# Block 3's keys and values from the context ahead of time, and four heads in a lone pass

## The chip, the cores and the metric

The kernel runs on one core of one Trainium2 chip. A core has five engines that run side by side: TensorE (PE, matrix products), VectorE (DVE), ScalarE (ACT), GpSimd (POOL) and SyncE (SP, which only issues transfers). [...] Products land in PSUM, everything else is in SBUF or in DRAM. The metric is the device time of one launch, in microseconds (us).

## The reference, cut to what matters

A batch of 8 sequences of 512 tokens, 256 features, goes through two layers, each an attention-like block and a feed-forward block, all gated by a tanh:

```python
x = x + tanh(g_xattn[0]) * mlstm(layernorm(x), ctx, ctx, ...)         # block 1: 8 heads of 32, decay matrix
x = x + tanh(g_ffn[0])   * attn_experts(layernorm(x), ...)            # block 2: self-attention, 32 heads of 8, then experts
x = x + tanh(g_xattn[1]) * cross(ctx, ctx, layernorm(x), mask, ...)   # block 3: 16 heads of 16
x = x + tanh(g_ffn[1])   * product_keys(layernorm(x), ...)            # block 4: top-8 of 4096 experts

def cross(k, v, q, mask, Wq, bq, Wk, bk, Wv, bv, Wo, bo):             # k = v = ctx
    qh = split_heads(q @ Wq + bq) / sqrt(16)
    kh, vh = split_heads(k @ Wk + bk), split_heads(v @ Wv + bv)
    scores = where(mask, einsum('bhqd,bhkd->bhqk', qh, kh), -inf)
    return einsum('bhqk,bhkd->bqhd', softmax(scores), vh).reshape(...) @ Wo + bo
```

The keys and values of block 3 depend on the context alone, not on `x`.

## The kernel before, in words

Everything is float32. The kernel has two stages: the attention stage (blocks 1 to 3, and the first products of block 4), which ends about 3078 us into the span, and the retrieval stage (the rest of block 4).

In the attention stage the sequences are taken in the order 0, 4, 1, 5, 2, 6, 3, 7 and are called m = 0 to 7. The two softmax attentions are cut into 24 *jobs*: ("A", m, f), f = 0 or 1, is half of block 2's heads of sequence m, ("C", m, 0) is block 3 of it. A job has 16 steps n = (g, c): group g of four heads, 128 rows c. Each job is passed twice. In the first pass (`maxima`) PE makes scores with queries on the partitions and DVE reduces them to row maxima (`nm`, L435). In the second pass (`exponentials`) PE makes the scores the other way round, with the maximum folded in as a further row of the operand, ACT takes the exponential from PSUM (`pr`, L463), and `values` multiplies with the values (`av`, L478). A head has at most 32 rows of operand, so four heads fit on PE's four groups of 32 rows and run side by side.

A hand-written planner interleaves the jobs. One round of its loop takes one step of the first pass of one job and one step of the second pass of the job before it, each in two half rounds. In a half round the first pass takes heads 2*half and 2*half + 1, the second the other two, so a full round always has four heads on PE. Each of the two passes takes one of the two score buffers in PSUM (`ps_sc`, two of 128 x 2 x 512) in a half round. Where one pass has no partner (the first job's maxima, the last job's exponentials, or a job that isn't ready), a half round has two heads alone. Between the score groups the planner hands PE time (`CREDIT`, in its own units) to *lanes*: generators that make the other blocks and say after each piece how much PE time it took or for how long they want to be left alone. The order of the lanes is their priority:

- `between` spreads a job's queries and keys from DRAM into the sets of operands `qa`, `ka` (`spread`);
- `after` closes block 3 (`leave`), and ends with `norm`;
- `before` makes block 1 (`cell`) and block 2's queries, keys and values (`queries`), in one lane for m = 0, 1, 3 to 7, and in a second lane, with borrowed tiles (`Lent`), for m = 2;
- `behind` makes the experts of block 2 (`experts`), then block 3's operands: `operands` projects keys from the context and queries from the stream, writes both to DRAM and spreads them; `values1` projects block 3's values straight into `v1`, after the block 3 before it has finished with `v1`;
- `fill` makes products of block 4 (`inner`, line L131) and has the lowest priority.

`weights2` fetches the projection weights of `behind` one ahead. `load_context` loads a transposed context into a tile "cT" (one buffer) on POOL's queue. The store tiles `pk`/`vk` share two buffers. PE's order is exactly the order of emission (`manual_schedule`); the order on the other engines is made by the framework's scheduler from the dependences.

Of the kernel before, what the change touches and what calls it, by code (L numbers as in the profile page):

```python
# [21 lines left out]
P = 128  # L22
# [14 lines left out]
def kernel(  # L37
# [142 lines left out]
    def attention_phase(ctx: ExitStack):  # L180
# [6 lines left out]
        wsp = ctx.enter_context(tc.tile_pool(name="wsp", bufs=2))  # L187
# [51 lines left out]
        class Weights:  # L239
# [20 lines left out]
        operand = [(w0, 3), (w3, 1), (w3, 0)]  # L260
        weights2 = Weights(
            "ws2", (M - 2) * (operand + [(w3, 2)]) + 2 * operand + 2 * [(w3, 2)], wsp
        )
# [56 lines left out]
        m_f = trp.tile([B * NC, P], F32, name="m_f", tag="pk", bufs=2)  # L320
        nc.vector.tensor_copy(m_f, m_u8)
# [3 lines left out]
        def constants():  # L325
# [8 lines left out]
            nc.vector.tensor_scalar(tbo, tbo, tg[:, 2:3], None, ALU.mult)  # L334
            mp = ps_m.tile([P, S], F32, name="mp", tag="m")
# [69 lines left out]
        class Attention:  # L405
            def __init__(self, m, qa, ka, va, first, hd):
                self.m, self.qa, self.ka, self.va = m, qa, ka, va
                self.first, self.hd = first, hd
                self.o = None

# [44 lines left out]
            def exponentials(self, n, half):  # L455
                g, c, jj = n // NC, n % NC, 1 - half
                if half == 0:
                    self.pr = [None, None]
                sc, product = self.pair(self.ka, self.qa, g, c, jj)

                def then():
                    self.pr[jj] = prb.tile([P, 2, S], F32, name="pr", tag="pr")
                    nc.scalar.activation(self.pr[jj], sc, AF.Exp)  # L463
                    if half == 1:
                        self.ready = (n, self.pr)

                return product, then

            def values(self):


                n, pr = self.ready
# [43 lines left out]
        xbs, cTs, lnx, qks, vds, xds, weights = {}, {}, {}, {}, {}, {}, {}  # L516
# [30 lines left out]
        class Tiles:  # L547
            user = ""

# [6 lines left out]
            def begin(self, m):  # L556
# [5 lines left out]
                nc.gpsimd.dma_start(qn, x[b].rearrange("(c p) d -> p c d", p=P))  # L562
                cT, ce = self.context(m)
                load_keys(nc.gpsimd, ce, b)
# [17 lines left out]
        class Lent(Tiles):  # L582
            user = "2"

# [13 lines left out]
            def context(self, m):  # L598
                return load_context(m, "cT"), self.cte
# [97 lines left out]
        def cell(m, own):  # L697
            b = order[m]
            qn, cT, ce = own.begin(m)
# [83 lines left out]
            if m == 0:  # L783
                all_pairs(qT, cT, ce, nM_d, aT, close)
            for pair in range(4) if m else ():
# [164 lines left out]
        def experts(m):  # L950
            Xb = xbs[m][:, :, :D]
            cTs[m] = load_context(m, "cTc" if m == M - 1 else "cT")
# [12 lines left out]
            w = weights2.get()  # L965
            for c in range(NC):
                ps = project(w, oT, c)
# [54 lines left out]

        def operands(m):
            Xb, cT = xbs[m][:, :, :D], cTs[m]
            b = order[m]
            xn = trp.tile([P, NC, D], F32, name="xn3", tag="t2")
# [4 lines left out]
            place, free = cross_set(m)  # L1031
            q1, k1 = sets[place]
            for i, srcT, dst in ((1, cT, k1), (0, nT, q1)):
                pd = drm.tile([D, S], F32, name="qk_d3")
                w = weights2.get()
                for n in range(NK):

                    def store(ps):
                        pk = trp.tile([P, S], F32, name="pk", tag="pk", bufs=2)
                        nc.vector.tensor_scalar(  # L1040
                            pk, ps, bqkv_sb[:, 2 * i + n : 2 * i + n + 1],
                            0.25 if i == 0 else 1.0, ALU.add, ALU.mult,
                        )
                        nc.sync.dma_start(pd[n * P : (n + 1) * P], pk)

                    yield from project_T(w, srcT, n, store)
                if i == 1:
                    yield ("rest", free)
                    mrow = m_dram[NC * b : NC * (b + 1)].rearrange("(o c) p -> o (c p)", o=1)
                    for j in range(4):  # L1050
                        for g in range(4):
                            nc.sync.dma_start(k1[32 * j + 16 : 32 * j + 17, g, :], mrow)
                    blank(q1)
                spread(dst, pd, 0, 16)

        def values1(m):
            b = order[m]
            vv = v1[:, :, : 16 * 17].rearrange("p c (h e) -> p c h e", e=17)
            w = weights2.get()
            for c in range(NC):  # L1060
                mk = m_key[:, NC * b + c : NC * b + c + 1]
                ps = project(w, cTs[m], c)
                nc.vector.tensor_scalar(
                    vv[:, c, :, 0:16], ps.rearrange("p (h e) -> p h e", e=16), mk, None, ALU.mult
                )
                nc.gpsimd.tensor_scalar(vv[:, c, :, 16], ones[:, :16], mk, None, ALU.mult)
                yield 1.0
# [132 lines left out]
        def before(sequences, tiles):  # L1200
            if tiles is Lent:
                yield ("rest", ("begun", 0))
            own = tiles()
            for m in sequences:
                Xa = yield from cell(m, own)
# [10 lines left out]
        def behind():  # L1216
            yield ("rest", ("lent", 0))
            for m in range(M):
# [10 lines left out]
                for n in (m,) if m < M - 2 else (m - 1, m) if m == M - 1 else ():  # L1229
# [627 lines left out]
```

## Time and profile before

| | |
|---|---|
| median of 3 runs | 3934.26 us (3929.36 to 3937.77) |
| the profiled execution's own time | 3939.58 us |
| its span | 3937.6 us |
| mean granted PE clock | 0.956 |
| attention stage | 0 to 3078 us |
| first job's maxima, alone | 114 to 255 us |
| last job's exponentials, alone | from 2921 us |
| PE busy | 3599.6 us |
| DVE busy | 2244.4 us |
| ACT busy | 1760.8 us |

The profile's page gives the busy time of each engine over the whole span; since the stages have different limits, the stretches between the planner's jobs are to be looked at one by one. The granted clock is the share of PE's full clock that it was given[...]. A busy PE includes matmuls that use only a part of its array.

### The profile page before, as it was taken

How to read it: one execution, taken by the hardware profiler on the slowest of the kernel's cores; microseconds unless marked ns; L12 is line 12 of the kernel's file. 1: busy time of each engine (PE TensorE's matmuls, PEld its weight loads, DVE VectorE, ACT ScalarE, POOL GpSimd, SP SyncE). 2: the span in 40 equal slices, each digit the busy share in tenths (PEclk: the TensorE clock that was granted, in tenths of full speed). 3: DMA queues.
4: the chain of work that ended last, by engine and by line, in shares of the span. 5: the costliest groups of instructions: out<-in, count | busy, mean ns of one | idle time of the engine just before them, and what ended most of it. 6: DMA issues, size and time to landing. Idle time of an engine off the chain costs nothing.

```text
span 3937.6 us, 76092 instructions
## 1 busy us (share of the span) xinstructions
PE 3599.6 (91%) x31049; PEld 1853.6 (47%) x31049; DVE 2244.4 (57%) x5483; ACT 1760.8 (45%) x2304; POOL 608.9 (15%) x645
## 2 busy tenths in 40 slices
PE   4898899898999999889999989988899999999998
PEld 1333344343343444334444434424344677777776
DVE  4546655655555554555444453455321589999993
ACT  2223544444444454444444443444244355555652
POOL 4003112111101110101100100010000133333331
PEclk7658999999999999999999999999899999999999
DMA  3203122131322332222332323220433443333331
GB/s 102 80 28 103 55 69 85 39 93 46 96 82 77 89 94 90 76 87 76 89 107 86 98 67 99 75 55 25 129 110 119 116 121 104 105 104 116 114 103 37
DMA packets 226249, 339.04 MB, mean 86 GB/s; under 512 B 30110, under 2 KB 175550, under 8 KB 217598
## 3 DMA queue, kind: packets, MB, share of 16 engines
q1 hardware_dynamic: 208476, 274.35, 23.5%
q0 software_dynamic: 16288, 59.25, 5.1%
q8 instruction: 244, 4.00, 0.4%
q14 instruction: 105, 0.86, 0.1%
q10 hardware_dynamic: 1136, 0.58, 0.1%
HBM read 236.66 MB, written 96.63 MB: 85 GB/s over the span
## 4 chain that ended last, share of the span: by engine, by line
PE 78%; DVE 11%; issue 3%; ACT 3%; DMA 2%; POOL 1%; SPq 0%; DVEq 0%; POOLq 0%; ACTq 0%
PE sc L417 22%; PE acc L1699 12%; PE ps_hd L131 10%; DVE nm L435 7%; PE av L478 7%; PE cf L1679 4%; PE ps_y L1003 3%; PE ps_sim L1431 3%; PE ps_p L366 3%; PE ps_q L377 3%; PE ps_h L984 3%; PE csc L826 2%; PE cav L811 1%; PE ps_hl L131 1%; PE ps_t L347 1%
## 5 line engine op out<-in xcount | busy, mean ns | idle before, releaser
L435 DVE TENSOR_REDUCE nm<-sc 128x2 f32<-128x1024 f32 x768 | 940.8, 1225 | 1046.5 <-PE sc L417 1045.8
L463 ACT ACTIVATE pr<-sc 128x1024 f32<-128x1024 f32 x768 | 786.1, 1024 | 999.0 <-PE sc L417 998.5
L417 PE MATMUL sc<-ka,qa 32*128 32x512 f32 x3072 | 974.1, 672 | 138.6 <-DVE nm L435 119.8
L417 PE MATMUL sc<-qa,ka 32*128 32x512 f32 x3072 | 899.8, 657 | 24.8 <-ACT pr L463 24.0
L417 PEld LDWEIGHTS sc<-ka,qa 32*128 32x128 f32 x3072 | 266.4, 191 | 527.5 <-DVE nm L435 310.7
L1699 PE MATMUL acc<-up_sb,gs 64*128 64x256 f32 x4096 | 468.4, 382 | 1.3 <-DVE gs L1688 1.3
L131 PE MATMUL ps_hd<-xT,dw 128*64 128x256 f32 x3584 | 430.5, 386 | 10.2 <-DVE pd L831 5.8
L478 PE MATMUL av<-pr,v 128*32 128x512 f32 x3072 | 424.4, 625 | 1.1 <-ACT pr L463 1.1
L1699 PEld LDWEIGHTS acc<-up_sb,gs 64*128 64x128 f32 x4096 | 390.0, 187 | 52.4 <-issue 4.7
L131 PEld LDWEIGHTS ps_hd<-xT,dw 128*64 128x64 f32 x3584 | 242.2, 137 | 233.1 <-issue 98.9
L1669 POOL TENSOR_TENSOR m<-o,cwT 128x1024 f32<-128x1024 bf16 x128 | 243.6, 1903 | 562.4 <-DVE o L1667 241.3
L417 PEld LDWEIGHTS sc<-qa,ka 32*128 32x128 f32 x3072 | 243.9, 187 | 80.2 <-ACT pr L463 54.2
L1163 ACT COPY hb<-ps_hd 128x512 f32<-128x512 f32 x224 | 131.3, 586 | 306.8 <-PE ps_hd L131 283.1
L478 PEld LDWEIGHTS av<-pr,v 128*32 128x32 f32 x3072 | 61.3, 109 | 305.1 <-issue 291.0
L804 ACT ACTIVATE pd<-mb,aT 128x256 f32<-128x256 f32 (+2 forms) x224 | 113.1, 553 | 184.8 <-PE cav L811 100.6
L1688 DVE TENSOR_TENSOR gs<-cf,gs 128x1024 f32<-128x1024 f32 x128 | 155.8, 1219 | 42.4 <-PE cf L1679 27.3
L1679 PE MATMUL cf<-m,m 64*64 64x64 f32 x8192 | 152.4, 222 | 0.8 <-DVE gs L1688 0.7
L1679 PEld LDWEIGHTS cf<-m,m 64*64 64x64 f32 x8192 | 134.8, 135 | 38.7 <-issue 38.3
L1665 ACT CAST m<-o 128x1024 f32<-128x1024 bf16 x128 | 133.7, 1045 | 39.3 <-DVE o L1663 35.5
L826 PE MATMUL csc<-qT,cT 32*128 32x512 f32 (+1 forms) x448 | 136.2, 537 | 12.3 <-DVE o L506 5.0
L984 PE MATMUL ps_h<-fT,w1e 128*128 128x256 f32 x512 | 133.7, 397 | 5.4 <-DVE o L506 4.8
L796 POOL TENSOR_SCALAR_AFFINE_SELECT mb<-mb 128x256 f32<-128x256 f32 x112 | 45.7, 408 | 581.7 <-ACT pd L804 347.1
(260 smaller groups left out, 4064.7 us busy)
## 6 DMA issues: line engine op xcount, KB each, us to landing
h_d<-hb SPq DMA_DIRECT2D x224, 256.0 KB
gs<-h_d SPq DMA_DIRECT2D x56, 1024.0 KB
dw<-in_down SPq DMA_DIRECT2D x112, 256.0 KB
qk_d<-pk SPq DMA_DIRECT2D x64, 256.0 KB
w1e<-in_w POOLq DMA_DIRECT2D x16, 1024.0 KB, 5.8
w2e<-in_w POOLq DMA_DIRECT2D x16, 1024.0 KB, 6.5
ws<-in_w SPq DMA_DIRECT2D x56, 256.0 KB
mb<-nM_d SPq DMA_DIRECT2D x28, 512.0 KB
```

The costliest lines, as they stand in the source:

```text
L131: nc.tensor.matmul(ps[64 * q : 64 * q + 64, :], dw[:, k, :], runs[:, :, q, :], start=(k == 0), stop=(k == NK - 1),)
L417: nc.tensor.matmul(sc[:, i, :], lhs[r : r + 32, g, c * P : (c + 1) * P], rhs[r : r + 32, g, :], start=True, stop=True,)
L435: newest = nc.vector.tensor_reduce(self.nm[:, c, 2 * half : 2 * half + 2, g], sc, AX.X, ALU.max, negate=True)
L463: nc.scalar.activation(self.pr[jj], sc, AF.Exp)
L478: nc.tensor.matmul(self.av[32 * j : 32 * j + 32, :], self.va[:, c, h * (self.hd + 1) : h * (self.hd + 1) + 32], pr[j // 2][:, j % 2, :], s ...
L826: nc.tensor.matmul(sc[i][:, s0:], cT[r : r + 32, g, s0 : s0 + P], qT[r : r + 32, g, s0:], start=True, stop=True,)
L984: nc.tensor.matmul(ps[:, :D], w1e[:, k, f * P : (f + 1) * P], fT[:, k, i * D : (i + 1) * D], start=(k == 0), stop=(k == NK - 1),)
L1665: nc.scalar.copy(m1, o1)
L1669: nc.gpsimd.tensor_tensor(m2, o2, tokens(cw), ALU.mult)
L1679: nc.tensor.matmul(cf[64 * q : 64 * q + 64, h, s, :], m2[rows, 4 * q + s // 2, :, s % 2], m1[rows, 4 * q + s // 2, :, s % 2], start=True, ...
L1688: nc.vector.tensor_tensor(gv, cf.rearrange("p h s i -> p i h s"), gv, ALU.mult)
L1699: nc.tensor.matmul(accs[n][q], gs[n % 2][rows, i, :], up_sb[rows, i, :], start=(i == 0), stop=(i == 63),)
```

## The change

Three things are changed together.

1. Block 3's keys and values of all sequences are projected in a lane of their own, `contexts`, above `fill` in priority: the keys of m = 0 to 3, then their values, and, after ("A", 1, 0), the keys and values of m = 4 to 7. They are kept in DRAM (`k_d3`, `v_d3`). `operands` now projects only the queries, then spreads both; `values1` becomes a lane that loads `v1` from DRAM. The weights `wo2` and `wq3` are kept in SBUF for the whole stage instead of being fetched for each use. The context is reloaded for each projection.
2. In a round with one pass alone (`alone`) both half rounds are issued as one, with four heads and both score buffers; the credit of both half rounds is given at once.
3. The second cell (m = 1) is made by the `Lent` lane, and m = 2 by the other. Its loads are issued at once, on SP's queue, and it goes on as soon as the first cell's products (`all_pairs`) are issued, not when the first maxima begin; once the first maxima have begun it stands ahead of the other lanes of `before` and `behind`. The cast of the mask is moved from the head of the stage into `constants`.

```diff
-        wsp = ctx.enter_context(tc.tile_pool(name="wsp", bufs=2))
+        wsp = ctx.enter_context(tc.tile_pool(name="wsp", bufs=1))
...
-        operand = [(w0, 3), (w3, 1), (w3, 0)]
-        weights2 = Weights(
-            "ws2", (M - 2) * (operand + [(w3, 2)]) + 2 * operand + 2 * [(w3, 2)], wsp
-        )
+        wo2, wq3 = (wsp.tile([P, NK, D], F32, name=name) for name in ("wo2", "wq3"))
+        for w, src in ((wo2, w0[3]), (wq3, w3[0])):
+            nc.sync.dma_start(w, src.rearrange("(k p) n -> p k n", p=P))
...
         nc.sync.dma_start(m_u8, mask)
-        m_f = trp.tile([B * NC, P], F32, name="m_f", tag="pk", bufs=2)
-        nc.vector.tensor_copy(m_f, m_u8)
...
             nc.vector.tensor_scalar(tbo, tbo, tg[:, 2:3], None, ALU.mult)
+            m_f = trp.tile([B * NC, P], F32, name="m_f", tag="pk", bufs=2)
+            nc.vector.tensor_copy(m_f, m_u8)
...
         class Lent(Tiles):
             user = "2"
+            loader = nc.sync
...
             def context(self, m):
-                return load_context(m, "cT"), self.cte
+                cT = exp.tile([P, NK, S], F32, name="cT2", tag="xT5", bufs=1)
+                self.loader.dma_start(cT, cxT[order[m]].rearrange("(k p) s -> p k s", p=P))
+                return cT, self.cte
...
                 all_pairs(qT, cT, ce, nM_d, aT, close)
+                rested.add(("pairs", 0))
...
+        def contexts():
+            for half in (range(M // 2), range(M // 2, M)):
+                for i in (1, 2):
+                    if i == 1 and half[0]:
+                        yield ("rest", ("A", 1, 0))
+                    w = wsp.tile([P, NK, D], F32, name="wkv", tag="wkv")
+                    nc.sync.dma_start(w, w3[i].rearrange("(k p) n -> p k n", p=P))
+                    for m in half:
+                        cT = load_context(m, "cT")
+                        yield ("wait", 5 if m or i > 1 else 25)
+                        for cost in (keys3, values3)[i - 1](m, w, cT):
+                            yield cost
+                            yield ("wait", 2)
+        def store3(pd, ps, n, i, scale):
+            pk = trp.tile([P, S], F32, name="pk", tag="pk", bufs=2)
+            nc.vector.tensor_scalar(
+                pk, ps, bqkv_sb[:, 2 * i + n : 2 * i + n + 1], scale, ALU.add, ALU.mult
+            )
+            nc.sync.dma_start(pd[n * P : (n + 1) * P], pk)
+        def keys3(m, w, cT):
+            pd = kds[m] = drm.tile([D, S], F32, name="k_d3", bufs=M)
+            for n in range(NK):
+                yield from project_T(w, cT, n, lambda ps: store3(pd, ps, n, 1, 1.0))
+            rested.add(("k_d", m))
+        def values3(m, w, cT):
+            pd = vcs[m] = drm.tile([P, NC, 16 * 17], F32, name="v_d3", bufs=M)
+            for c in range(NC):
+                mk = m_key[:, NC * order[m] + c : NC * order[m] + c + 1]
+                ps = project(w, cT, c)
+                pk = trp.tile([P, S], F32, name="vk", tag="pk", bufs=2)[:, : 16 * 17]
+                heads = pk.rearrange("p (h e) -> p h e", e=17)
+                nc.vector.tensor_scalar(
+                    heads[:, :, 0:16], ps.rearrange("p (h e) -> p h e", e=16), mk, None, ALU.mult
+                )
+                nc.gpsimd.tensor_scalar(heads[:, :, 16], ones[:, :16], mk, None, ALU.mult)
+                nc.sync.dma_start(pd[:, c], pk)
+                yield 1.0
+            rested.add(("vc_d", m))
...
+            pd = drm.tile([D, S], F32, name="q_d3")
+            for n in range(NK):
+                yield from project_T(wq3, nT, n, lambda ps: store3(pd, ps, n, 0, 0.25))
+            yield ("rest", ("k_d", m))
+            yield ("rest", free)
+            mrow = m_dram[NC * b : NC * (b + 1)].rearrange("(o c) p -> o (c p)", o=1)
+            for j in range(4):
+                for g in range(4):
+                    nc.sync.dma_start(k1[32 * j + 16 : 32 * j + 17, g, :], mrow)
+            blank(q1)
+            spread(q1, pd, 0, 16)
+            spread(k1, kds[m], 0, 16)
...
             if tiles is Lent:
-                yield ("rest", ("begun", 0))
-            own = tiles()
+                loaded = own.begin(sequences[0])
+                yield ("rest", ("pairs", 0))
...
-                for n in (m,) if m < M - 2 else (m - 1, m) if m == M - 1 else ():
-                    yield ("rest", ("C", n - 1, 0))
-                    yield from values1(n)
-                    ready.add(("v1", n))
+
+        def values1():
+            for m in range(M):
+                yield ("rest", ("C", m - 1, 0))
+                yield ("rest", ("vc_d", m))
+                nc.sync.dma_start(v1[:, :, : 16 * 17], vcs[m])
+                ready.add(("v1", m))
...
-        lanes += [Lane(before((0, 1, *range(3, M)), Tiles)), Lane(behind()), Lane(before((2,), Lent))]
-        lanes.append(Lane(fill()))
+        lanes += [Lane(before((0, *range(2, M)), Tiles)), Lane(behind()), Lane(before((1,), Lent))]
+        lanes += [Lane(contexts()), Lane(fill())]
...
+                if ("begun", 0) in rested:
+                    first.insert(3, lanes[5])
...
-            for half in range(2):
+
+            alone = bool(one) != bool(two)
+            for halves in ((0, 1),) if alone else ((0,), (1,)):
                 work = []
-                if one:
-                    work.append(live[one[0]].maxima(one[1], half))
-                if two:
-                    work.append(live[two[0]].exponentials(two[1], half))
+                for half in halves:
+                    if one:
+                        work.append(live[one[0]].maxima(one[1], half))
+                    if two:
+                        work.append(live[two[0]].exponentials(two[1], half))
...
-                spent = beside(credit + CREDIT[half])
-                now += max(RETURN, used + CREDIT[half] + credit - spent)
+                new = sum(CREDIT[half] for half in halves)
+                spent = beside(credit + new)
+                now += max(RETURN * (1.5 if alone else 1.0), used + new + credit - spent)
```

## The prediction

> **What bounds the kernel now.** I read the page first, then the windows view cut where the planner's jobs begin, then the waits of PE in the late stages, then the timeline of lone rounds.
>
> ```profile
> PE 3599.6 (91%) x31049; PEld 1853.6 (47%) x31049; DVE 2244.4 (57%) x5483; ACT 1760.8 (45%) x2304; POOL 608.9 (15%) x645
> PEclk7658999999999999999999999999899999999999
> PE 78%; DVE 11%; issue 3%; ACT 3%; DMA 2%; POOL 1%; SPq 0%; DVEq 0%; POOLq 0%; ACTq 0%
> L435 DVE TENSOR_REDUCE nm<-sc 128x2 f32<-128x1024 f32 x768 | 940.8, 1225 | 1046.5 <-PE sc L417 1045.8
> ```
>
> TensorE (PE) carries 78% of the chain of waits and is the bound of the whole attention stage; VectorE (DVE) is second. But the clock row is low in its first four digits: there PE work costs almost double.
>
> ```profile
> 0.00:114.00 114.00, 50.78 (x230) 26.62 (x230) 42.54 (x106) 26.12 (x52) 44.26 (x69) 0.81 0.43 119
> 114.00:255.00 141.00, 126.48 (x344) 43.40 (x344) 76.18 (x130) 36.45 (x66) 12.12 (x28) 0.56 0.15 41
> 255.00:384.00 129.00, 108.43 (x563) 38.23 (x564) 73.30 (x140) 46.05 (x65) 30.27 (x41) 0.83 0.26 77
> 384.00:495.00 111.00, 99.39 (x589) 36.33 (x584) 68.13 (x105) 55.95 (x79) 18.82 (x31) 0.94 0.22 61
> 2553.00:2645.00 92.00, 76.00 (x534) 28.65 (x536) 47.33 (x55) 37.05 (x42) 12.18 (x11) 0.98 0.28 77
> 2645.00:2780.00 135.00, 112.28 (x641) 54.09 (x634) 61.71 (x87) 53.58 (x54) 6.51 (x9) 0.96 0.15 38
> 2780.00:2921.00 141.00, 133.08 (x888) 60.22 (x888) 54.66 (x78) 51.16 (x64) 3.70 (x8) 0.95 0.37 120
> 2921.00:3078.00 157.00, 153.11 (x1044) 79.02 (x1046) 28.68 (x66) 61.37 (x93) 5.75 (x6) 1.00 0.40 121
> 161.00:252.00 91.00, 86.75 (x236) 30.94 (x238) 46.48 (x81) 23.73 (x48) 8.66 (x21) 0.50 0.11 38
> 338.00:419.00 81.00, 72.21 (x442) 31.15 (x438) 50.74 (x84) 36.78 (x48) 25.73 (x33) 1.00 0.40 112
> ```
>
> Columns: stretch, length, busy time of PE, weight loads, DVE, ScalarE (ACT), GpSimd (POOL), granted clock, DMA share, GB/s. From 114 to 255 the first job's maxima run alone: 16 rounds take 141 us, where 16 rounds of both passes take 111 to 117 later. The second lone stretch is the last job's exponentials from 2921.
>
> ```profile
> 198.11 2.08 PE L417 MATMUL sc<-ka,qa 32*128 32x512 f32 x4
> 2976.86 1.13 PE L417 MATMUL sc<-qa,ka 32*128 32x512 f32 x4
> 2978.92 1.13 PE L417 MATMUL sc<-qa,ka 32*128 32x512 f32 x4
> 2978.04 1.02 ACT L463 ACTIVATE pr<-sc 128x1024 f32<-128x1024 f32 x1 [0.43 <-PE sc L417]
> 27.17 0.21 DVE L321 CAST m_f<-m_u 32x128 f32<-32x128 uint8 x1 [15.24 <-DMA m_u<-in_mask]
> 92.70 2.21 PE L347 MATMUL ps_t<-ident,xn 128*128 128x128 f32 x8 [13.42 <-DVE xn L880]
> cT<-in_cxT POOLq DMA_DIRECT2D x12, 512.0 KB, 4.4
> PE sc L417 <- DVE nm L435: 10.1, 16, 1.3
> ```
>
> A lone half round is two heads (x4 records) and takes 1.13 us at full clock, 2.08 at half. A half round of both passes is four heads on four row groups and takes the same time (1.14 in the chain). So a lone round pays twice for half the work.
>
> **The change, part by part.** The sum is made against the profiled execution: span 3937.6, its own time 3939.6, which is 5.3 above the median of 3934.3. The order of the built program gives the counts; PE has the same matmuls before and after. Retrieval (3078 to the end, 859 us) has the same order and counts as zero; so do the renamed weight tiles and the weight loads that fall away, DMA being busy a third.
>
> *Four heads in a lone round.* The planner makes 22 rounds with maxima alone and 22 with exponentials alone, before and after. Each loses one score interval: 1.04 us at full clock, 2.0 at half. 44 of them are 46 us at full clock; 17 lie in the slow stretch at the start, the other 27 nearly all after 2314.
>
> *Keys and values moved.* 16 key projections (8 records, about 1.8 us) and 32 value projections (0.87 from start to start) leave the later stages and go in two halves, into the planner's rounds up to 39 and 83 to 129 (of some 430). Nothing is saved by that alone. 32 values now pass through the two "pk" buffers to DRAM and come back in 8 loads; SP and DMA have room; a "pk" write that must wait for its store holds DVE, and with it the next reduction and then PE's scores. The Lent cell now has sequence 1, its loads stand on SP, and it begins during sequence 0's cell.
>
> *Stage 0 to 114.* The mask cast leaves DVE's head, where it held the first layernorm from 12 to 27 us. Mask, Lent loads and "wkv" now stand on SP behind the ones_d wait, so nM_d leaves SP about 8 us earlier; the key projection put before the "at" transposes eats 5 of that: gain 3. Then six key units, a transpose set and four gate matmuls (15 us at full clock) stand before the transposes of xn, where PE idled 13.4. Each key pair needs the single "cT" buffer refilled by POOL: PE must finish, POOL issue (0.7), 4.4 us land (7.3 in the first 60 us); POOL's reciprocal roots for xn are queued behind that issue. I take two uncovered refills: loss 15. Net +12, between 0 (the idle 13.4 covers all but two) and +25 (half clock throughout).
>
> *Stage 114 to 255.* PE busy 126.5 at 0.56 is 70 us of full-clock work. Off: 16 score intervals (17) and about 11 of the cell begun earlier; on: 12 value projections (10). Left: 52. At half clock that is 104. Which clock? [...] Two heads use half the array. [...] the clock will flip as in 262 to 338 (mean about 0.75): 52/0.75 = 69. [...] A lone round still needs two reductions of 1.225 in series on both score buffers: at least 1.1 + 2.45 = 3.6 a round, 57 in all, and DVE's whole work is 76 - 9 (moved) + 12 x 0.48 (values) = 73. At 90% DVE use: 81. I take 93, with refills of cT and half-clock stretches: -48, between -30 (half clock, 104 plus waits) and -62.
>
> *Stage 255 to 384.* Four value projections and the cell's remainder come on (+7 us), a fuller array helps the clock: 0, +-10. *Stage 384 to 495.* 15 us of the cell's products are already done; the floor of DVE's rounds (two of 1.225 plus 1.1 each, 78 in 16 rounds) stays below: -13, between -6 and -16.
>
> *Stages 495 to 2314.* The order shifts about 8.6 us of PE work (filler and the second half of the keys) into these stages; they cost about 1.1 times their work: +8. Unknown waits (pk buffers, SP order, refills in rounds 83 to 129) put it between -15 and +30.
>
> *From 2314.* Values of the last two sequences no longer stand in the way: three of the four empty rounds ahead of the last exponentials go, and the last maxima overlap one pass more. Work per stage falls, counted in the order: 3 in 2438:2553; 11 in 2553:2645, of which the DVE floor (5.1 a round, 82) lets 8 through; 8 in 2645:2780; 20 in 2780:2921 plus 7 of waits; 6 in the last. -3 -8 -9 -27 -5 = -52, between -30 and -65. The last queries' spread now follows 20 small DMAs (mask rows, zeros), about 0.35 us each on SP, after the q projection: the wait of 9.1 us on qa<-qk_d stays.
>
> Sum: 12 - 48 + 0 - 13 + 8 - 52 = -93. 3939.6 - 93 = 3846.6; on the median's scale 3841.
>
> **The rivals.** *B, the wait moves to the reader of PSUM.* Both score buffers belong to one pass, so PE in a lone round waits for two reductions or two exponentials. If first-stage rounds stay at half clock (-33 instead of -48) and the 16 last rounds wait as long as they saved (20 of the 52 lost): -58, 3876. For: the 10.1 us above, PE waiting for nm where filler is scarce. Against: in the last stage ACT needs 2 x 1.02 a round beside about 3.9 us of PE filler. 18%.
>
> *C, slower: the single cT buffer.* 16 refills in series with PE's order: 0.7 + 4.4 to 7.3 us each, 82 to 128, if no other PE work is put between. I counted about 17 already; +105 gives 3946, slower. It decides from about 7 us uncovered on each of 16. Against: in the later half some 16 rounds of other work lie among the eight refills. 5%.
>
> *D, more.* The clock opens early, the first lone stage runs at DVE's bound (78), the next gains 15, the start loses nothing: 3796. 7%.
>
> The forecast itself gets 70%. That the change does nothing is excluded: the order shows four heads together.
>
> **How the numbers follow.** Independent bounds (12, 16, 10, 6, 22, 17) give about 36 as a root of squares; taking in most of B and the edge of D: 3795 to 3898. About 0.2%, 8 us, is what a measurement can tell here: slower by more is most of C, 0.04; same 0.03; faster 0.93.
>
> **What would show it.** First scores at 120 to 135 instead of 113.9; first lone stage 85 to 100 us at a clock near 0.75; lone groups x8 of 1.1 us; attention done near 2985. Wrong if the first lone stage is over 110 or its clock stays 0.5; if PE's waits on "cT" or "wkv" DMAs exceed 30 us; if stages from 495 on grow by over 30.

## The result and the profile after

Timed beside each other, the changed kernel took 3873.43 us (median of 4, 3867.09 to 3878.41) and the kernel before 3932.60 us: a ratio of 0.9847, 95% interval 0.9826 to 0.9869. It is faster by 1.5%, 59 us. The forecast was faster, at 3841 in a range of 3795 to 3898: the range holds the result, but a third of the expected 93 us did not come. The profiled execution has a span of 3876.6 us, 61.0 less than before.

The page of the kernel after, its engine row, its clock row, the rows of the reduction and of the scores, and the refills of the context:

```profile
PE 3534.1 (91%) x31049; PEld 1847.7 (48%) x31049; DVE 2247.1 (58%) x5487; ACT 1755.9 (45%) x2301; POOL 607.4 (16%) x647
PEclk8789999999999999999999999999999999999999
L435 DVE TENSOR_REDUCE nm<-sc 128x2 f32<-128x1024 f32 x768 | 938.9, 1225 | 988.8 <-PE sc L417 988.1
L417 PE MATMUL sc<-ka,qa 32*128 32x512 f32 x3072 | 929.4, 667 | 155.7 <-DVE nm L435 146.5
L417 PE MATMUL sc<-qa,ka 32*128 32x512 f32 x3072 | 874.4, 655 | 16.3 <-ACT pr L464 14.6
cT<-in_cxT POOLq DMA_DIRECT2D x22, 512.0 KB, 4.9
```

PE has the same 31049 matmuls and is busy 65.5 us less (3599.6 before), while it is idle for about as long (338 and 342 us): more of the work runs side by side on the array, and at a higher clock (0.966 in the mean, 0.956 before). The second and third digits of the clock row were 6 and 5. The context is now loaded 24 times instead of 16: 22 times on POOL's queue, as the last line says, and twice on SP's (15 and 1 before).

The windows of the kernel after, cut at the same jobs as before (columns as in the prediction):

```profile
0.00:130.00 130.00, 77.12 (x322) 44.81 (x326) 56.73 (x135) 32.65 (x62) 43.24 (x68) 0.81 0.56 153
130.00:235.00 105.00, 85.15 (x334) 35.73 (x330) 68.24 (x110) 24.65 (x45) 14.32 (x35) 0.77 0.27 74
235.00:369.00 134.00, 115.84 (x613) 44.57 (x616) 75.53 (x145) 50.12 (x73) 35.23 (x52) 0.89 0.25 79
369.00:466.00 97.00, 77.16 (x483) 26.97 (x475) 57.84 (x82) 43.48 (x54) 12.30 (x17) 0.95 0.26 64
2530.00:2616.00 86.00, 64.75 (x452) 21.41 (x456) 45.78 (x53) 34.44 (x38) 12.17 (x11) 0.98 0.17 47
2616.00:2738.00 122.00, 103.71 (x605) 48.63 (x598) 58.64 (x81) 52.86 (x53) 5.15 (x5) 0.96 0.12 31
2738.00:2858.00 120.00, 111.76 (x804) 47.88 (x807) 49.62 (x63) 48.02 (x59) 1.27 (x2) 0.95 0.41 135
2858.00:3015.00 157.00, 150.38 (x1122) 85.45 (x1115) 34.69 (x81) 61.34 (x96) 6.81 (x7) 1.00 0.44 135
```

The first lone stage takes 105 us instead of 141 and its clock is 0.77 instead of 0.56. The stages ahead of the last lone one are shorter by 6, 13 and 21. The last lone stage has kept its length: PE is busy there nearly as long as before (150 against 153 us), with 78 more matmuls (1122 against 1044).

Lone rounds in the timeline of the kernel after, the first job's:

```profile
151.99 2.09 PE L417 MATMUL sc<-ka,qa 32*128 32x512 f32 x8
165.88 1.14 PE L417 MATMUL sc<-ka,qa 32*128 32x512 f32 x8
168.68 1.12 PE L417 MATMUL sc<-ka,qa 32*128 32x512 f32 x2 [0.81 <-DVE nm L435]
171.89 2.08 PE L417 MATMUL sc<-ka,qa 32*128 32x512 f32 x6 [2.09 <-DVE nm L435]
```

Four heads (x8) take 2.09 us at half clock and 1.14 at full clock, as two heads did (2.08 and 1.13). The last two lines are one round in which the second score buffer came free later than the first: its group is torn in two and pays twice. In two more of the 16 rounds the group is torn in the same way, its second half beginning 0.05 us after the second reduction ends. The first round is torn too, but has no reduction ahead of it.

### The profile page after: what moved, and what is told of

Read it like the earlier page. It is cut to its first block, busy times and chain, and to the rows that moved or that the text cites. A ratio compares the mean times of both kernels' runs of the same rounds, so it can differ in the third digit from the quotient of the medians.

```text
span 3876.6 us, 76238 instructions
## 1 busy us (share of the span) xinstructions
PE 3534.1 (91%) x31049; PEld 1847.7 (48%) x31049; DVE 2247.1 (58%) x5487; ACT 1755.9 (45%) x2301; POOL 607.4 (16%) x647
## 5 line engine op out<-in xcount | busy, mean ns | idle before, releaser
L464 ACT ACTIVATE pr<-sc 128x1024 f32<-128x1024 f32 x768 | 783.3, 1023 | 991.2 <-PE sc L417 990.7
L417 PE MATMUL sc<-ka,qa 32*128 32x512 f32 x3072 | 929.4, 667 | 155.7 <-DVE nm L435 146.5
L417 PE MATMUL sc<-qa,ka 32*128 32x512 f32 x3072 | 874.4, 655 | 16.3 <-ACT pr L464 14.6
L417 PEld LDWEIGHTS sc<-ka,qa 32*128 32x128 f32 x3072 | 253.9, 190 | 525.5 <-DVE nm L435 335.1
L131 PE MATMUL ps_hd<-xT,dw 128*64 128x256 f32 x3584 | 431.8, 387 | 11.4 <-DVE pd L839 5.3
L812 ACT ACTIVATE pd<-mb,aT 128x512 f32<-128x512 f32 (+1 forms) x224 | 113.3, 553 | 138.8 <-PE cav L819 71.7
L834 PE MATMUL csc<-qT,cT 32*128 32x512 f32 (+1 forms) x448 | 125.0, 499 | 18.9 <-DVE o L508 6.0
```

Of the source, the lines that this page charges most:

```text
L131: nc.tensor.matmul(ps[64 * q : 64 * q + 64, :], dw[:, k, :], runs[:, :, q, :], start=(k == 0), stop=(k == NK - 1),)
L417: nc.tensor.matmul(sc[:, i, :], lhs[r : r + 32, g, c * P : (c + 1) * P], rhs[r : r + 32, g, :], start=True, stop=True,)
L464: nc.scalar.activation(mine[jj], sc, AF.Exp)
```

## Experiments

First the whole table, so that each experiment can be read against the others. Times are from the profiled execution of each; a region begins with the first scores of its first job. "Early" ends where the job ("A", 1, 1) begins, "middle" where ("A", 7, 0) begins, "late" with the attention stage.

| kernel | median, us | ratio to before, 95% interval | early | middle | late | retrieval |
|---|---|---|---|---|---|---|
| before | 3934.26 | 1 | 495.4 | 1818.8 | 764.3 | 859.0 |
| after | 3873.43 | 0.9847 (0.9826 to 0.9869) | 466.2 | 1832.0 | 716.5 | 861.9 |
| cell_only: part 3 | 3943.64 | 1.0013 (0.9998 to 1.0029) | 483.1 | 1831.3 | 763.4 | 860.7 |
| lone_only: part 2 | 3904.87 | 0.9897 (0.9865 to 0.9928) | 503.6 | 1796.3 | 744.5 | 859.1 |
| lone_cell: parts 2, 3 | 3912.20 | 0.9931 (0.9909 to 0.9953) | 459.2 | 1846.2 | 740.5 | 859.3 |
| after_pairs: parts 1, 3 | 3899.72 | 0.9891 (0.9866 to 0.9916) | 491.5 | 1815.4 | 741.6 | 861.5 |
| no_cell: parts 1, 2 | 3929.79 | 0.9970 (0.9954 to 0.9987) | 528.8 | 1821.2 | 716.1 | 858.6 |
| late_keys | 3871.23 | 0.9819 (0.9787 to 0.9851) | 466.2 | 1822.0 | 721.2 | 862.4 |
| own_ctx | 3889.34 | 0.9871 (0.9840 to 0.9902) | 470.8 | 1836.0 | 721.3 | 859.2 |
| late_pool | 3858.28 | 0.9815 (0.9801 to 0.9829) | 454.0 | 1823.9 | 721.0 | 857.6 |
| late_act | 3867.39 | 0.9829 (0.9809 to 0.9848) | 454.4 | 1829.5 | 721.7 | 858.2 |
| after_again | 3880.09 | 0.9847 (0.9831 to 0.9863) | 476.7 | 1828.9 | 720.8 | 858.1 |
| late_pool_again | 3864.95 | 0.9817 (0.9802 to 0.9832) | 457.2 | 1823.5 | 720.4 | 862.0 |

The row of before has its first three runs; each ratio was taken against runs of before on the same chip, whose medians lie between about 3933 and 3941, so ratios compare better than medians. A ratio is made from the runs themselves and can differ by 0.2% from the quotient of the medians (lone_only: 0.9915). The pair after and after_again is one kernel profiled twice: 10.5 us apart in the early region, 3 to 4 in the others. Smaller differences between two single profiles are read as nothing.

### Which part brings what

Four kernels have one part or two. Part 2 alone, put on the kernel before:

```diff
-            for half in range(2):
+            alone = bool(one) != bool(two)
+            for halves in ((0, 1),) if alone else ((0,), (1,)):
...
```

> The kernel before with part 2 alone (four heads in a lone round); keys, values and cells as before. Theory (the gain is the score interval that each lone round loses, worth double where the clock is half, and the rest of the change only makes room): first scores stay at 114; the first lone stage falls from 141 to about 75 to 85 us at a clock of 0.7 or more; but sequence 1 is then not ready, the order shows 6 more rounds with exponentials alone in the second stage, so that stage grows from 128 to about 165; the late stages lose 15 to 25. In all -40 to -55 (about 3883). Rival (the early keys and values carry the gain): under -20, above 3912, with the first lone stage no shorter than 120.

Measured: 0.9897, some 34 us by the medians and 41 by the ratio, at or under the lower end of what was expected. The first lone stage fell to 92 us at a clock of 0.61, short of the expected 75 to 85 at 0.7, and the stage after it rose from 129 to 192, not 165:

```profile
116.00:208.00 92.00, 73.48 (x236) 26.52 (x236) 61.98 (x91) 23.24 (x39) 7.58 (x16) 0.61 0.20 46
208.00:400.00 192.00, 155.59 (x757) 56.12 (x756) 92.42 (x179) 69.57 (x100) 35.07 (x52) 0.78 0.18 56
```

The first job ends earlier, sequence 1 isn't ready, and six more lone rounds fill the gap. The early region is no better than before; the gain is in the middle and late. Part 2 holds two things, the four heads in one group and the planner's changed credit, which no run separates.

Part 3 alone:

```diff
-Lane(before((0, 1, *range(3, M)), Tiles)), Lane(behind()), Lane(before((2,), Lent))]
+Lane(before((0, *range(2, M)), Tiles)), Lane(behind()), Lane(before((1,), Lent))]
...
+                if ("begun", 0) in rested:
+                    first.insert(2, lanes[4])
```

> The kernel before with part 3 alone (mask cast moved, second cell on the Lent lane and begun during the first); two heads in a lone round. Theory: first scores about 108 to 112, the first lone stage still 135 to 145 us near half clock since its two-head rounds fill half the array; in all -5 to -15 (about 3922). Rival (the early second cell itself is the gain): -30 or more, with the second stage under 115 us.

Measured: 1.0013, no gain. The second cell is indeed done sooner, but inside the first lone stage, most of it at half clock, and the stage grows from 141 to 157 us:

```profile
112.00:269.00 157.00, 126.74 (x378) 44.31 (x380) 79.10 (x144) 35.66 (x68) 20.34 (x37) 0.56 0.19 51
```

What the early region gained (12) the middle gave back (13). The expectation of 5 to 15 was wrong.

Parts 2 and 3 together, the two edits above:

> Parts 2 and 3 without part 1: block 3's keys and values projected where they were before. Theory: first scores 108 to 114, first lone stage 75 to 88, no extra lone rounds, third stage begins at about 315 to 330 instead of 384 (369 with part 1); late stages as in the kernel with part 2 alone; in all -65 to -85 (about 3858), that is faster than the full change by 5 to 25, since the full change lost 16 us ahead of the first scores. Rival (part 1 earns its keep in the late stages): slower than the full change, above 3885.

Measured: 0.9931, not the 3858 expected, and the rival was right. Early is now 36 better than before, the middle 27 worse. The first lone stage takes 107 us where 75 to 88 were expected, with the clock at 0.64 and PE idle for 28 us:

```profile
112.00:219.00 107.00, 79.17 (x275) 29.88 (x276) 62.28 (x95) 24.44 (x45) 8.78 (x21) 0.64 0.20 49
```

So the early keys and values are not a ballast that the other two parts carry, as that theory had it.

The kernel after without part 2 (parts 1 and 3):

```diff
-            for halves in ((0, 1),) if alone else ((0,), (1,)):
+            for halves in ((0,), (1,)):
...
-RETURN * (1.5 if alone else 1.0)
+RETURN
```

> The changed kernel with two heads in a half round of a lone pass again (part 2 undone). Theory: the first lone stage goes back to 135 to 150 us with a clock near 0.55, the last lone stage grows by 15; 45 to 65 slower than the changed kernel, near 3925 to 3935. Rival (part 1 and 3 carry half): 3900 or less. [...]

Measured: 0.9891, where 3925 to 3935 was expected and the rival was right: parts 1 and 3 alone carry 1.1%, some 40 us. 23 of them are late, where the keys and values of the last sequences are no longer made.

The kernel after without part 3 (parts 1 and 2):

```diff
-                if ("begun", 0) in rested:
-                    first.insert(3, lanes[5])
...
-Lane(before((0, *range(2, M)), Tiles)), Lane(behind()), Lane(before((1,), Lent))]
+Lane(before((0, 1, *range(3, M)), Tiles)), Lane(behind()), Lane(before((2,), Lent))]
```

> The changed kernel without part 3 (cells and mask cast as before): parts 1 and 2. The order shows 7 more rounds with exponentials alone in the second stage, sequence 1 not being ready. Theory (time is PE's work, the same 2457 us here as in the changed kernel, plus waits and half clock; a lone round of four heads costs PE nothing extra): those rounds are filled with other work that then lacks nothing later; within 10 us of the changed kernel, 3866 to 3886. Rival (without the early second cell the planner runs dry and seven rounds of 5 us are lost): 3900 or more.

(The Lent cell keeps its own tile for the context here.) Measured: 0.9970; again the rival was right. Part 3, worth nothing by itself, is worth about 1.2% here. In the windows of this kernel the stage after the first lone one shows why:

```profile
134.00:232.00 98.00, 78.74 (x285) 31.61 (x284) 66.87 (x104) 23.79 (x39) 14.33 (x32) 0.74 0.28 77
232.00:415.00 183.00, 155.40 (x786) 56.97 (x784) 94.70 (x185) 69.26 (x98) 35.41 (x54) 0.82 0.20 61
```

It has 23 rounds, seven of them with exponentials alone, since sequence 1 is again not ready, and takes 183 us against 134 in after. The late region is that of the kernel after (716). So the parts don't add up in the same way everywhere. Late they do: 764 to 742 by part 1 (with 3), to 717 with part 2 as well. Early, parts 2 and 3 need each other: part 2 alone loses 8, part 3 alone gains 12, together they gain 36. With part 1 on top the gain is 29 (19 in the repetition), although PE does some 29 us more work in this region (297 against 268, an estimate with time at half clock counted half, since in before PE went on 2.01 us after the start of a group of two heads there, and 1.06 at full clock); the clock is at half for 184 us of it in lone_cell, for 140 in after and for 164 in its repetition. Part 1 alone was not run.

### What sets the clock in the first lone stage

after_pairs leaves the first lone stage at 0.65. In the next kernel, made from after_pairs, the other two heads of each lone half round are computed as well, and their scores thrown away ("the gate" in its expectation stands for the granted clock):

```diff
+                    if alone:
+                        work.append(live[(one or two)[0]].idle_pair((one or two)[1], half, not one))
...
+            def idle_pair(self, n, half, second):
+                g, c = n // NC, n % NC
+                lhs, rhs = (self.ka, self.qa) if second else (self.qa, self.ka)
+                _, product = self.pair(lhs, rhs, g, c, half if second else 1 - half)
+                return product, lambda: None
```

> The changed kernel with pairs in lone rounds, and in each lone half round the other two heads are computed as well and thrown away: the same score intervals for PE as with pairs, but the whole array filled. Output as in the changed kernel. If the gate follows the share of the array that works: first lone stage at a clock of 0.78 or more and 115 to 128 us, against 0.65 and 138 with pairs. If it follows how busy PE is: 0.65 and about 138 again, since PE's intervals are the same.

The same stage in the windows of after_pairs and, below, of this kernel:

```profile
130.00:267.00 137.00, 123.42 (x394) 49.78 (x391) 79.27 (x142) 30.37 (x57) 19.51 (x43) 0.65 0.24 70
```

```profile
130.00:255.00 125.00, 108.07 (x519) 46.16 (x520) 80.28 (x143) 29.48 (x55) 19.88 (x44) 0.89 0.27 77
```

PE issues 125 matmuls more, is busy for a smaller share of the stage (108/125 = 86% against 90%), and gets 0.89 of the clock instead of 0.65. The stage is 12 us shorter with work added that nobody uses. So in this stage the granted clock followed how much of the array works, not how busy PE is. Each has one profile, but the differences (0.24 and 12 us) are far above those of the two profiles of after in its first lone stage (0.77 and 0.73; 105.4 and 109.3 us). One time of the whole kernel was taken, 3909.47; it says nothing more, since all lone rounds carry the extra work.

### What ends the start and the first lone stage

The first scores come 16 us later than before, because all eight key projections of the first half were put ahead of them. In late_keys these begin only when the first maxima have:

```diff
-                    if i == 1 and half[0]:
-                        yield ("rest", ("A", 1, 0))
+                    if i == 1:
+                        yield ("rest", ("A", 1, 0) if half[0] else ("begun", 0))
```

> The changed kernel with the first half of the keys and values begun only when the first maxima begin. Takes away the eight key projections ahead of the first scores (14.5 us at full clock, in the way of sequence 0). Theory: first scores at 112 to 117 instead of 129.6; the moved work comes back in the second and third stage (6 and 8 us more work there); in all 2 to 8 faster than the changed kernel, about 3868. Rival (the projections ahead of the first scores are free because PE idles there): first scores still 125 or later, same time. Second rival (their work kept the clock up): first lone stage longer by 10 or more and no gain.

The first scores come at 103.7 instead of 129.6, and yet ("A", 1, 1) begins at 466.2, as in after (476.7 in its repetition). The 26 us went in two ways: the first lone stage became 14.5 us longer, most of it a new wait of 11.2, and the two stages after it 11.4 longer, where the moved projections now lie. The expectation had put 14 us of moved work there and no such wait. In time late_keys is not separated from after (0.9787 to 0.9851 against 0.9826 to 0.9869). In this kernel's timeline, the second cell's running maximum on its way out to DRAM and back, and PE's second group of scores of that cell:

```profile
86.24 0.26 SPq L746 DMA_DIRECT2D nM_d<-pd  x1
112.86 0.35 SPq L796 DMA_DIRECT2D mb<-nM_d  x1
121.34 0.41 POOL L804 TENSOR_SCALAR_AFFINE_SELECT mb<-mb 128x256 f32<-128x256 f32 x1 [9.04 <-DMA mb<-nM_d]
123.28 2.25 PE L834 MATMUL csc<-qT,cT 32*128 32x384 f32 x4 [11.22 <-DVE pd L839]
```

The store leaves at 86; the load of it back stands on SP's queue behind the stores of queries and values and the spreads of the first job, and is issued at 112.9; for the values alone (`vk`) SP waits 7.0 us on the way. The first scores of that cell stay in their PSUM buffers until DVE has multiplied them with the decay made from it (L839), and PE stands 11.2 us for those buffers. (In the kernel after the load is issued at 123.7 and covered by the later start.)

A second try at the same start kept the first keys early but took them from contexts already in SBUF:

```diff
-                        cT = load_context(m, "cT")
+                        if i == 1 and m == 2:
+                            yield ("rest", ("begun", 0))
+                        cT = held[m] if i == 1 and m < 2 else load_context(m, "cT")
```

> The changed kernel, but the keys of sequences 0 and 1 are projected from the contexts that their cells already hold in SBUF, and those of 2 and 3 wait for the first maxima: no refill of the single context buffer ahead of the first scores, half of the work there. Theory: first scores at 116 to 121 (7 us of work less and the waits of 6.8 on the refills gone), 5 to 12 faster than the changed kernel, about 3864. Rival (the refills cost nothing): no difference, 3873.

Slower than expected: 0.9871 (0.9840 to 0.9902), no faster than after. First scores at 107.4, but the same wait of 11.0 us for the decay (its load was issued at 116.3). Neither theory nor rival foresaw that.

If that queue is the cause, the store and the first load on another queue must free it. The edit is made on late_keys:

```diff
+            side = nc.gpsimd if m == 1 else nc.sync
-            nc.sync.dma_start(nM_d, nM)
+            side.dma_start(nM_d, nM)
...
-                nc.sync.dma_start(mb, nM_d[2 * pair : 2 * pair + 2].partition_broadcast(P))
+                (side if pair == 0 else nc.sync).dma_start(mb, nM_d[2 * pair : 2 * pair + 2].partition_broadcast(P))
```

> The kernel after with the first half of the early keys begun only at the first maxima (as in late_keys), and with sequence 1's negated running maximum (nM_d) and the first load of it back as a decay operand (mb) on GpSimd's queue instead of SyncE's. In late_keys that store left at 86.2 us but SyncE issued the load only at 112.9, behind the stores of queries and values and the spreads, the select ran at 121.3, and PE stood 11.2 us at 123.3 for the decay. Theory (the second cell's chain through SyncE's queue is what sets the end of the first lone stage): the select runs at 95 to 100, the wait of 11 us goes, the first lone stage is 105 to 110 instead of 119.9, the job A11 starts at about 455 instead of 466.2, and the time is 3859 to 3865 (late_keys 3871). Rival 1 (the lone stage is bound by VectorE's reductions and by buffers, so another wait takes its place): stage 116 to 120, A11 at 463 to 467, time 3869 to 3873. Rival 2 (the early stages get shorter, but the middle gives it back as it did for lone_cell): A11 at 455, the middle 1832 or more, time 3870 or more.

> As late_pool, but the store and the first load stand on ScalarE's queue, behind its own activations. ScalarE then waits about 4 us for the store to land before its copies of the values, so theory: the same gain less what that wait costs the value copies, 3860 to 3868; rival 1: 3869 to 3875; rival 2: A11 earlier by about 10 but the time as in late_keys.

(late_act has nc.scalar in place of nc.gpsimd.) In the timeline of late_pool, where the lines below the edit are numbered one higher:

```profile
88.88 0.56 POOL L797 DMA_DIRECT2D mb<-nM_d  x1 [1.93 <-ACT pk L906]
94.01 0.41 POOL L805 TENSOR_SCALAR_AFFINE_SELECT mb<-mb 128x256 f32<-128x256 f32 x1 [4.57 <-DMA mb<-nM_d]
111.88 1.96 PE L835 MATMUL csc<-qT,cT 32*128 32x384 f32 x3
```

The load goes out 24 us sooner, PE's matmuls of csc no longer stand for it, the stage takes 105.6 us instead of 119.9 and ("A", 1, 1) begins at 454.0 (454.4 in late_act, 457.2 in a second profile of late_pool). The select ran at 94.0, and two other queues in place of SP's give the same early gain: the theory of the queue is confirmed for the early region. The middle gave nothing back in late_pool and some 7 us in late_act, which took 3867.39 us, within its expected 3860 to 3868.

The timed ratios don't separate late_pool from late_keys (0.9815 and 0.9819), and they were timed on different chips. So the last two runs put late_pool beside after:

> The kernel after, unchanged, once more beside late_pool on one chip, because late_keys and late_pool were timed beside runs of before that differ by about 8 us (3941 and 3933), as much as is in dispute. If late_pool is truly faster than after by the 10 to 12 us that its early stages show: ratio to before here about 0.985 and late_pool's about 0.982, with 10 to 15 us between the medians. If the 15 us between the earlier medians were the chip: less than 5 us between them here.

> late_pool, unchanged, beside after_again on one chip: 10 to 15 us under after_again if the shorter early stages hold to the end, under 5 us if the middle gives them back. The job A11 again starts at about 454 us in its profile.

Measured on one chip: before 3938.86, after 3880.09, late_pool 3864.95, as expected. The gap of 15.1 us equals that of the earlier medians (3873.43 and 3858.28). late_pool beats both kernels, at 0.9817 (0.9802 to 0.9832) of before. The 15 us belong to the later keys and the other queue together: what the queue alone brings to the whole time stays unmeasured, since late_keys was not timed beside late_pool.

## Why the prediction was right, and where a third of the gain went

Working against the profiled executions, step by step, with after_again's value where it bears on it:

| step | predicted | measured | in after_again |
|---|---|---|---|
| start, to the first scores | +12 | +15.7 | +16.7 |
| first lone stage | -48 | -35.9 | -32.0 |
| the stage after it | 0 | +5.1 | +8.8 |
| the next | -13 | -14.0 | -12.2 |
| 495 to 2314 of before | +8 | +13.2 | +10.1 |
| from 2314 to the end of attention | -52 | -47.8 | -43.5 |
| retrieval | 0 | +2.9 | -0.9 |
| sum | -93 | -60.8 | -53.0 |

The sums are those of the spans but for rounding (-61.0 and -53.0). Of the 32 us that did not come, 12 are missing in the first lone stage; the others miss 3 to 5 each, except "the next", which gained one more than forecast. Of the signs named in advance, the first scores, the clock of 0.75 and the groups x8 came; the first lone stage (105 us, 85 to 100 forecast) and the end of attention (3015, 2985 forecast) came late. No mark of being wrong was reached: PE waited 10.1 us for "cT" and "wkv", and the stages from 495 on did not grow by 30.

**The start: near in size, wrong in its parts, and so partly luck.** Fifteen us were booked for uncovered refills of "cT". PE's waits from 0 to 130 in the kernel after:

```profile
PE ps_t L346 <- DVE qn L107: 12.7, 1, 12.7
PE ps_p L365 <- DMA cT<-in_cxT: 6.8, 2, 5.5
PE mp L335 <- DVE m_f L333: 5.6, 1, 5.6
PE csc L834 <- ACT vk L920: 5.3, 2, 4.9
```

Two refills were uncovered, as predicted, but they cost 6.8. The moved mask cast, booked at nothing but a gain, now holds PE for 5.6 (L333). late_keys shows what the early keys cost here in all: 26 us of start.

**The first lone stage: the term that failed.** The clock was foreseen (0.75; 0.77 and 0.73 measured), and so were the waits (24; PE is idle for 20). What was too small is the work: 69 us of busy PE were predicted, 85.2 are measured. From the prediction's 70 us at full clock, 17 were to go for the scores, 11 for the cell, and 10 to come. The groups of PE in that stage, before and then after:

```profile
L417 PE MATMUL sc<-ka,qa 32*128 32x512 f32 x128 | 62.1, 1015 | 5.5 <-issue 3.2 <-DVE nm L435 2.2
L826 PE MATMUL csc<-qT,cT 32*128 32x512 f32 (+3 forms) x76 | 40.4, 793 | 1.9 <-ACT em L751 1.8
```

```profile
L417 PE MATMUL sc<-ka,qa 32*128 32x512 f32 x132 | 32.0, 911 | 2.9 <-DVE nm L435 2.9
L376 PE MATMUL ps_q<-wkv,cT 128*128 128x256 f32 x48 | 18.7, 526 | 10.6 <-DVE pd L839 10.6
L834 PE MATMUL csc<-qT,cT 32*128 32x384 f32 (+3 forms) x58 | 21.3, 599 | 6.5 <-ACT vk L920 4.9 <-DVE pd L839 1.2 <-DVE hk L783 0.4
```

The work can be estimated from these records: with busy time at half clock counted half, and overlapping time once, to the matmul that began first, the stage held 68.6 us of work before (70 in the prediction). The scores went from 29.5 to 19.4: 10 saved where 17 were booked. The prediction took one score interval of 1.04 off each of 16 rounds; but before, 32 intervals took 29.5 and not 33.3, part of them lying under other matmuls, and after, 16 rounds took 19.4 and not 16.6, torn ones paying twice. The cell gave up 9 of the 11, and the value projections cost 12.5, not 10. So 62 us of work remained instead of 52 (61 in after_again). At the forecast clock of 0.75 these ten are 13 of the 16 us that PE was busy longer; the rest is that the clock was lower while PE was busy (62 us of work in 85) than in the mean of the stage. The waits, 4 under the estimate, gave back a little. The value projections also wait 10.6 us (L376): they want a PSUM buffer of the tag "m", which the cell's scores hold until DVE has read them (L839). This wait was not named in the prediction.

**The clock.** The prediction went by the trace of before: PE was busy 95% of the stretch 161 to 252 and had 0.50, and busy 89% of 338 to 419 and had 1.00. That the half-filled rounds of two heads keep the clock low was its author's estimate. after_pairs and pairs_full bear it out for the first lone stage: with two heads in a lone half round PE was busy 90% of it and had 0.65, with four it was busy 86% and had 0.89. But the prediction put the higher clock down to the four heads, and they alone did not bring it: the stage had 0.56 before, 0.61 in lone_only and 0.64 in lone_cell, 0.65 with the value projections and pairs of heads (after_pairs), and 0.77 and 0.73 (0.74 in no_cell) only with both. So the number was right for half of a reason. How the clock depends on the share of the array outside these stages was not shown.

**Late.** The mechanism and nearly the size were right, and after_pairs splits it: 23 for keys and values made early, 25 for four heads. Two terms were off. In the stage ahead of the last lone one (-27 predicted, -21.4 measured) PE was busy 21.3 us less, the 20 that were booked as work, but the 7 of waits did not go: for `nm` PE waited 7.6 us before and 8.1 after. And the last lone stage did not lose 5 but 0.4. Its score groups, before and then after:

```profile
L131 PE MATMUL ps_hd<-xT,dw 128*64 128x256 f32 x636 | 74.5, 383 | 1.1 <-ACT hb L1163 0.9
L417 PE MATMUL sc<-qa,ka 32*128 32x512 f32 x128 | 33.8, 640 | 0.0
L377 PE MATMUL ps_q<-wo,oT 128*128 128x256 f32 x16 | 3.7, 386 | 0.0
```

```profile
L131 PE MATMUL ps_hd<-xT,dw 128*64 128x256 f32 x688 | 79.1, 382 | 3.7 <-DMA dw<-in_down 2.2 <-ACT hb L1190 0.9 <-ACT xT L355 0.5
L417 PE MATMUL sc<-qa,ka 32*128 32x512 f32 x128 | 20.1, 640 | 0.4 <-ACT pr L464 0.4
L376 PE MATMUL ps_q<-wo,oT 128*128 128x256 f32 x32 | 7.7, 389 | 0.0
```

The scores gave up 13.7 us there. The stage kept its length because work from the stages ahead moved in: 52 more products of block 4, and the output projection of a second sequence. That is a shift and no loss; those stages are shorter for it. The wait for the last queries' spread, said to stay at 9.1, fell to 5.0.

**Middle.** The prediction booked 8.6 us of PE work here, at a little more than its cost, and left waits open. The middle's rows, before and then after:

```profile
495.00:2314.00 1819.00, 1684.77 (x10960) 737.44 (x10957) 975.05 (x1469) 835.49 (x1016) 224.76 (x305) 0.98 0.29 82
466.00:2298.00 1832.00, 1697.62 (x11032) 744.85 (x11032) 986.79 (x1497) 849.18 (x1044) 227.84 (x315) 0.98 0.28 81
```

PE is busy 12.9 us longer, and idle for the same time, 134.2 and 134.4: the waits in all did not grow. Weighted by the clock as above, 3.7 of the 13 us are work; the other 9 come from half clock, which lasts 82 us here instead of 65 (79 in after_again). Between the extremes of the experiments, lone_only with 1796 and lone_cell with 1846, the 50 us are 16 of work, 16 of half clock (51 us of it and 96) and 18 of waits. Why one order of work meets half clock more often than another was not tested.

**The rivals.** B's number, 3876, was met, but not by its mechanism: the clock of the first stage rose, and in the last rounds PE waited 0.4 us for ScalarE (L464), not 20. That the number fits is luck. Its core, the reader of the two buffers, is seen only in three torn rounds of the first job and two of the last, whose groups took 2.05 us instead of 1.14: it had some force, less than B gave it. C is dead: 6.8 us of refills in the start and none that matter later. D did not come; late_pool has the start without loss that it supposed, and 3858 us.

**Slips in the prediction's own sums.** None of them moves the forecast of 3841. The stretch 262 to 338, named for a mean of about 0.75, has 0.71. The bound of -30 leaves 7 us of waits beside 104 of work, where the forecast itself has 24. Rival C's 105 is the middle of 82 and 128 with nothing taken off for the 17 already counted; with them off it is 88, and C comes to 3929, a little faster than before. DVE's floor of 16 rounds of two reductions and two score intervals is 74 us, not 78, and D's steps add up to 3799, not 3796. The 12 loads of the context are those between 300 and 3000 us, of 16 in all.

## What to carry to other kernels

Before a phase is made shorter, look at what must be ready when it ends: here the faster lone round and the early keys, without the second cell begun early, ran into seven more lone rounds and lost nearly all, while the early cell alone brought nothing. Test parts in pairs, not only alone. And follow a small transfer that stands on a critical chain through its queue: the load that reads a 16 KB store back was issued 24 us late, behind other transfers in the same queue that waited for their inputs, and moving two lines to another queue let the early stages end 12 us sooner (454 in late_pool against 466 in late_keys).

## What the runs showed of the hardware

Adding discarded matmuls that fill the other half of the array made a stage faster: 125 us at a granted clock of 0.89 in pairs_full against 137 at 0.65 in after_pairs, with PE busy 86% and 90%. And the clock makes one kernel differ from itself: after and its repetition have 0.77 and 0.73 in the first lone stage, 0.95 and 0.91 in the third after the start, and are 10.5 us apart when the job ("A", 1, 1) begins. PE's work up to there is the same (297 and 296 us, weighted by the clock as above) and its idle time nearly so (111 and 109); half clock lasted 140 us in one and 164 in the other.
